# Row-phase order for the conv results, the residual and the identity of a two-layer conv kernel

## The chip, the cores and the metric

The kernel runs on one core of a Trainium2 chip. The metric is the device time of one execution in microseconds (us). The kernel before took 3264.07 us, the median of three runs (3260.51 to 3272.7).

A core has a tensor engine (PE in the profile, with its weight loads shown apart as PEld), a vector engine (VectorE, DVE), a scalar engine (ScalarE, ACT), GpSimd (POOL) and a sync engine (SP) that here only issues transfers (DMAs). Each runs its own list of instructions in order and waits on semaphores of the others. The transfers of all queues run on the same 16 DMA engines.

## The reference, cut to what matters

The input x is 4 images of 128 channels x 128 x 128 pixels, float32. Two layers follow each other.

The first layer has an attention over 9 x 9 overlapping 16 x 16 regions per image (step 14) with a residual; the overlaps are averaged. Its result is called `xf`. Then:

```python
y = _ln(xf, ln2_g, ln2_b)
y = y @ w_p0 + b_p0                      # 128 -> 256 channels
ym = conv5x5_depthwise(ym, dw_k)         # padding 2
ym = batch_norm(ym)                      # mean and variance over all images and pixels
y = gelu(gelu(ym)) @ w_p2 + b_p2         # 256 -> 128 channels
x = y + xf
```

The second layer keeps its input as identity:

```python
identity = x
out = act_quant(x)                       # clip to 0..1, 15 levels
out = conv3x3(out, weight_quant(w1))
out = act_quant(batchnorm(out, gamma1, beta1))
out = conv3x3(out, weight_quant(w2))
return batchnorm(out, gamma2, beta2) + identity
```

(The names are shortened from the reference; both batch norms need the statistics of the whole batch before any of their output can be formed.)

## The kernel before, in words

The order of the work on PE, ScalarE, VectorE and SP is the order in which the kernel's Python calls are made (`manual_schedule`); no planner moves instructions there. Channels lie on the 128 partitions. The line numbers are those of the kernel before.

**Attention and depthwise conv.** The attention runs over 36 bands of 16 rows. `beside(t)` (L881) lays the projections of the neighbouring bands and pieces of the depthwise conv between the attention's products. `post_chunks` (L528) ends a band: the merged rows go out to the memory tensor `xf_d` (through the list of stores that L431 issues on SP), the first 256-channel projection goes to `y2_d`, split into even and odd columns. Two tiles per half hold that projection on its way out, so ScalarE must wait for a store to land before it reuses one.

The depthwise conv (`conv_steps`, L614, matmuls in `depthwise`, L600) is a banded product. An image's 128 rows are cut into groups g of 16 rows. Partitions of its result are four channels times 32 values m = 2 ro + e, where ro is the row within the group and e says even or odd column; the free dimensions are the groups and the 64 columns x of that parity. So one result tile holds, for one (ro, e), the rows ro, ro + 16, ro + 32 and so on. Those of one ro are called a row phase here. `products` (L640) copies the result from PSUM, takes statistics, and stores it to `cv_d`. `conv_rest` (L678) does the last two groups of the last image when the attention is over; it has its own store loop (L729). `cv_d` is `[group, channel, (m, x)]`, so that a partition of the tile is written as one piece of 64 values (256 B) for each group.

**GELU stage** (`gelu_stage`, L1187). It works by units of 1024 pixels; there are 64, 16 per image, and a unit is eight neighbouring rows. For each: SP loads `cv` (1 MB, L1199) and `xfl` (0.5 MB, L1208), ScalarE does the batch norm with the first GELU and then the second GELU (L1216, L1219), PE projects (L1228), VectorE adds the residual and the even and odd columns fall back into place (L1236), GpSimd clips, VectorE quantises into a padded 8-bit image `q1[b]` of 130 x 130 (L1246, `to_int`, L1176). The identity goes to `id_d`. Two units behind, `conv3x3` (L1157) runs the first 3x3 conv: 18 matmuls per unit, nine for each half of four rows; tap t has its row offset dy = t // 3. `stats_of` (L1172) takes the statistics, `keep` (L1249) copies the result to `c1_d`, or, for the last image, to the on-chip tile `c1_s`.

**Last stages** (`last_stages`, L1287). The statistics pass (loop at L1317): unit n is loaded, normalised with Relu on ScalarE (L1328), and the second 3x3 conv of unit n - 3 runs on PE. On VectorE the calls stand in this order:

```python
                    pc = conv3x3(ps_d, n - 3, wq[1])
                    stats_of(st2, n - 3, pc)
...
                        nc.vector.tensor_scalar(a[:, px], a[:, px], 15.0, ROUND, ALU.min, ALU.add)
                        to_int(rows_in(q1[b], k)[:, h], a[:, px])
```

so the quantisation of unit n (L1340, L1176) comes after the statistics of the conv of unit n - 3. The conv result itself is dropped, except for the last image, whose results overwrite `c1_s`. Once the statistics are complete, the output pass (L1346) does the conv again for three images, applies the batch norm (ScalarE, L1350), adds the identity loaded from `id_d` up to eight units ahead (VectorE, L1351) and stores to `out` (L1354). Four PSUM tiles and four `z` tiles take turns.

Of the kernel before, what the change touches and what calls it, by code (L numbers as in the profile page):

```python
# [14 lines left out]
P = 128  # L15
# [14 lines left out]
N_TAPS = 25  # L30
MAX_SCORE = 64.0
GR = 16
CW = P // 2
KD = 2 * (GR + 4)
NCK = 8
# [11 lines left out]
def layers(  # L47
# [40 lines left out]


    y2_d = [dram.tile([P + 4, 2, 2 * P, CW], F32, name=f"y2_d{b}") for b in range(B)]  # L90
    cv_d = [dram.tile([P // GR, 2 * P, GR * P], F32, name=f"cv_d{b}") for b in range(B)]

    dw_d = dram.tile([2 * NCK, KD, 3, 16 * 32], F32, name="dw_d")
    pad_d = dram.tile([2 * GR + 3, 7, 2 * P], F32, name="pad_d")
# [90 lines left out]
    with ExitStack() as actx:  # L185
# [342 lines left out]
        def post_chunks(t, sel=None):  # L528


            b, i = bands[t]
            chunks = []
            for at, (r, n) in enumerate(finished(t)):
                held = {}
                squares, variance, deviation, spread, scaled = normalise(
                    lambda n=n, held=held: held["xf"][:, : n * P], n * P, sel
                )

                def project(hh, r=r, n=n, at=at, held=held):
                    if hh == 0:  # L540
                        held["xf"] = xfp.tile([P, LB * P], F32, name="xf")
                    px = slice(hh * n // 2 * P, (hh + 1) * n // 2 * P)
                    pm = ps_m.tile([P, 512], F32, name="pm")
                    po = pm[:, : n // 2 * P]
                    nc.tensor.matmul(po, wo, rows_of(ob[t], r + hh * n // 2, n // 2), start=True, stop=True)  # L545
                    nc.vector.scalar_tensor_tensor(
                        held["xf"][:, px], po, bo, xr[t, at][:, px], ALU.add, ALU.add
                    )
                    if hh:
                        store(  # L550
                            xf_d[b][:, (i * STEP + r) * P : (i * STEP + r + n) * P],
                            held["xf"][:, : n * P],
                        )
# [60 lines left out]
        def conv_steps(n, ahead=2):  # L614
# [25 lines left out]
            def products(at):  # L640
                k, jj, c0 = tiles[at]
                ut, wt = U.pop(at), W[k, jj]
                pc = [ps_m.tile([P, nj, ng, CW], F32, name="pm") for _ in range(2)]
                depthwise(pc, wt[:, :, c0:], ut, nc_)
                for half in range(2):
                    cv = cp.tile([P, nj, ng, CW], F32, name=f"c{half}")
                    nc.scalar.copy(  # L647
                        cv.rearrange("p j g x -> p (j g x)"), pc[half].rearrange("p j g x -> p (j g x)")
                    )
                    for j in range(nj):  # L650
                        nc.vector.bn_stats(  # L651
                            st0[:, k, half, 2 * jj + c0 // 4 + j, n, :], cv[:, j].rearrange("p g x -> p (g x)")
                        )
                        ch = 32 * k + 16 * half + 8 * jj + c0 + 4 * j
                        store(
                            bass.AP(
                                cv_d[b].tensor,
                                cv_d[b][g0, ch, 0:1].offset,
                                [[CW, P], [2 * P * GR * P, ng], [1, CW]],
                            ),  # L660
                            cv[:, j],
                        )

            def begin():
# [13 lines left out]
        def conv_rest(n, w_t, u_t, c_t):  # L678
# [32 lines left out]
            def step(k):  # L711
# [6 lines left out]
                for half in range(2):  # L718
# [6 lines left out]
                            st0[:, k, half, j, n, :], cv[:, j].rearrange("p g x -> p (g x)")  # L725
                        )
                    engine = (nc.sync, nc.scalar)[half]
                    for g in range(ng):
                        engine.dma_start(  # L729
                            out=bass.AP(  # L730
                                cv_d[b].tensor,
                                cv_d[b][g0 + g, 32 * k + 16 * half, 0:1].offset,
                                [[CW, P], [4 * GR * P, 4], [1, CW]],
                            ),
                            in_=cv[:, :, g],
                        )

            def run_all():
                for k in range(4):
# [400 lines left out]
    def padded(pool, name):  # L1140
        q = pool.tile([P, QW, QW], F8, name=name)
        nc.gpsimd.memset(q[:, 0, :], 0.0)
        nc.gpsimd.memset(q[:, QW - 1, :], 0.0)
        nc.gpsimd.memset(q[:, 1 : QW - 1, 0:1], 0.0)
        nc.gpsimd.memset(q[:, 1 : QW - 1, QW - 1 :], 0.0)
        return q

    U = 2 * RB * P
    units = [(b, k) for b in range(B) for k in range(NU2)]

    def pixels(k):
        return slice(k * U, (k + 1) * U)

    def rows_in(q, k):
        return q[:, 1 + 2 * RB * k : 1 + 2 * RB * (k + 1), 1 : 1 + P]

    def conv3x3(pool, n, w):  # L1157
        b, k = units[n]
        pc = pool.tile([P, 2, RB, P], F32, name="pc")
        for h in range(2):  # L1160
            r = (2 * k + h) * RB
            for t in range(9):
                dy, dx = divmod(t, 3)
                nc.tensor.matmul(  # L1164
                    pc[:, h], w[:, t, :], q1[b][:, r + dy : r + dy + RB, dx : dx + P],
                    start=(t == 0), stop=(t == 8),
                )
        return pc.rearrange("p h r c -> p h (r c)")
# [18 lines left out]
    def gelu_stage():  # L1187
        with (
# [7 lines left out]
            def load(n):  # L1196
# [1 line left out]
                cv = ld.tile([P, 2, U], F32, name="cv")  # L1198
                nc.sync.dma_start(  # L1199
                    out=cv,  # L1200
                    in_=cv_d[b][k // 2].rearrange("(h p) n -> p h n", p=P)[:, :, pixels(k % 2)],
                )
                loaded[n] = [cv]

# [16 lines left out]
            def second_projection(n):  # L1221
# [12 lines left out]
                pb_ = pb.rearrange("p m n -> p (m n)").rearrange("p (r e c) -> p r e c", e=2, c=P // 2)  # L1234
# [12 lines left out]
                to_int(rows_in(q1[b], k), a)  # L1247

            def keep(n, pc):  # L1249
                b, k = units[n]  # L1250
# [9 lines left out]
            gelus(0)  # L1260
            before1()
            before2()
            for n in range(len(units) + 2):
                if n + 2 < len(units):
                    load(n + 2)
                    load_xf(n + 2)
# [10 lines left out]
                if n >= 2:  # L1277
                    stats_of(st1, n - 2, pc)
                    keep(n - 2, pc)
                if n == len(units) - 1:  # L1280
                    most1()
            for out_, in_ in stores:
# [4 lines left out]
    def last_stages():  # L1287
        with (
# [18 lines left out]
                    nc.sync.dma_start(out=firsts[n], in_=c1_d[b][:, pixels(k)])  # L1307

            def load_id(at):
                b, k = units[order[at]]  # L1310
# [6 lines left out]
            for n in range(len(units) + 3):  # L1317
# [10 lines left out]
                        nc.scalar.activation(a[:, px], a[:, px], AF.Relu, bias=sh1, scale=sc1)  # L1328

                if n >= 3:  # L1330
                    b, k = units[n - 3]
# [12 lines left out]
            sc2, sh2 = rest2()  # L1344
            stores = []
            for at, n in enumerate(order):  # L1346
                b, k = units[n]
# [59 lines left out]
```

## Time and profile before

| | |
|---|---|
| median of three runs | 3264.07 us |
| span of the profiled execution | 3262.4 us |
| PE busy | 3089.8 us (95%), 30,954 matmuls |
| VectorE, ScalarE, GpSimd busy | 2018.7, 1991.5, 837.6 us |
| moved by DMA | 680.65 MB in 809,828 packets |
| packets under 512 B, under 2 KB, under 8 KB | 580,919, 695,936, 809,472 |
| mean rate | 209 GB/s |

The profiled execution's own time is its span, within 1.7 us of the median of the runs. Busy PE time is the time in which a matmul is under way; matmuls are pipelined, so a busy PE isn't PE at its peak. The counts of packets are cumulative: 580,919 of the 809,828 carry less than 512 B. The profile also cuts the span into 40 slices of 81.6 us, where a digit is the busy share in tenths, and it can be asked for any window. A line such as "PE pm L600 <- DMA u<-y_d: 16.6, 6, 5.4" says that PE's work of line 600 waited for that transfer 16.6 us in all, 6 times, at most 5.4 us.

### The profile page before, as it was taken

To read this page: it belongs to the slowest core of one execution; us is meant where nothing else is said; L and a number is where in the kernel's file an instruction comes from. 1 tells how busy PE (TensorE), PEld (TensorE's weight loads), DVE (VectorE), ACT (ScalarE), POOL (GpSimd) and SP (SyncE) were. 2 spreads that over 40 slices of the span, in tenths; PEclk is the share of its full clock that TensorE was granted. 3 is DMA by queue.
4 is the path that set the end of the run, shared out by engine and by line. 5 is a ranking of instruction groups with operands and counts; after the bars stand their busy time and mean duration, and the time that the engine had idled before them with its cause. 6 is when DMAs were issued, how large, how long until landed. Compare 5 with 4: busy or idle time off the path is not lost.

```text
span 3262.4 us, 75716 instructions
## 1 busy us (share of the span) xinstructions
PE 3089.8 (95%) x30954; PEld 1544.8 (47%) x30954; DVE 2018.7 (62%) x3244; ACT 1991.5 (61%) x2658; POOL 837.6 (26%) x1058
## 2 busy tenths in 40 slices
PE   8999999999999999999989998876899999999998
PEld 4555554544544444544444444443544444444443
DVE  5877887776766667676655564542555555666543
ACT  5777776777776776767655564532467777433443
POOL 3444443333333333333322232211111111000000
PEclk9999999999999999999999998877699999999999
DMA  3555677888886888886889988857899999552398
GB/s 82 150 165 159 170 185 183 192 210 198 208 200 160 193 202 204 197 209 166 188 203 207 201 199 187 191 158 199 245 359 358 357 359 306 169 167 84 106 357 312
DMA packets 809828, 680.65 MB, mean 209 GB/s; under 512 B 580919, under 2 KB 695936, under 8 KB 809472
## 3 DMA queue, kind: packets, MB, share of 16 engines
q1 hardware_dynamic: 798879, 669.17, 75.6%
q8 instruction: 247, 4.05, 0.5%
q0 software_dynamic: 1024, 3.93, 0.4%
q10 hardware_dynamic: 9568, 2.61, 0.3%
q14 instruction: 110, 0.89, 0.1%
HBM read 408.72 MB, written 270.79 MB: 208 GB/s over the span
## 4 chain that ended last, share of the span: by engine, by line
PE 80%; DMA 7%; issue 4%; ACT 4%; SPq 3%; DVE 3%; POOL 0%; ACTq 0%; DVEq 0%; POOLq 0%
PE pc L1164 21%; PE pm L600 9%; PE sc L784 9%; PE po L847 8%; PE pm L493 7%; PE pb L1228 7%; PE pm L561 5%; PE pm L770 4%; PE po L855 4%; DMA y_d<-y 3%; PE pm L377 3%; PE pm L545 3%; ACT pt L792 2%; DVE rd L867 1%; DMA u<-y_d 1%
## 5 line engine op out<-in xcount | busy, mean ns | idle before, releaser
L867 DVE RECIPROCAL rd<-po 128x256 f32<-128x256 f32 x324 | 569.3, 1757 | 447.6 <-PE po L855 444.7
L792 ACT ACTIVATE pt<-sc 128x1024 f32<-128x1024 f32 x648 | 628.0, 1024 | 128.2 <-PE sc L784 62.6
L1164 PE MATMUL pc<-q,wq 128*128 128x512 fp8e4 x3168 | 699.0, 380 | 5.1 <-DVE q L1176 5.1
L802 POOL TENSOR_TENSOR sm<-pt 128x512 f32<-128x512 f32 x324 | 413.2, 1275 | 1058.2 <-ACT pt L792 718.3
L1164 PEld LDWEIGHTS <-wq 128*128 128x128 fp8e4 x3168 | 308.7, 97 | 405.7 <-issue 37.0
L784 PE MATMUL sc<-q,kr 32*128 32x256 f32 x5184 | 403.3, 414 | 22.5 <-ACT pt L792 22.2
L600 PE MATMUL pm<-u,w 40*32 40x504 f32 (+5 forms) x7680 | 372.0, 505 | 45.6 <-DMA u<-y_d 22.5
L784 PEld LDWEIGHTS sc<-q,kr 32*128 32x128 f32 x5184 | 249.6, 190 | 261.8 <-issue 166.7
L847 PE MATMUL po<-pt,v 128*32 128x256 f32 x5184 | 358.9, 396 | 5.5 <-DVE part L871 4.7
L647 ACT COPY c<-pm 128x512 f32<-128x512 f32 (+1 forms) x256 | 132.3, 563 | 280.2 <-PE pm L600 249.4
L561 PE MATMUL pm<-xn,wp 128*128 128x512 f32 (+1 forms) x576 | 250.1, 565 | 38.1 <-ACT y L566 37.5
L566 ACT ACTIVATE y<-pm,vectors 128x512 f32<-128x512 f32 (+1 forms) x288 | 182.9, 641 | 152.4 <-DMA y_d<-y 98.3
L802 DVE TENSOR_TENSOR sm<-pt 128x512 f32<-128x512 f32 x324 | 243.7, 752 | 29.8 <-ACT pt L792 29.8
L600 PEld LDWEIGHTS pm<-u,w 40*32 40x32 f32 x7680 | 146.4, 112 | 229.9 <-issue 163.3
L493 PE MATMUL pm<-xn,wqkv 128*128 128x512 f32 (+1 forms) x576 | 248.5, 560 | 2.7 <-ACT v L775 2.0
L651 DVE BATCH_NORM_STATS2 st<-c 128x6 f32<-128x512 f32 (+2 forms) x320 | 160.9, 550 | 142.1 <-ACT c L647 141.7
L1228 PE MATMUL pb<-cv,wp 128*128 128x512 f32 x512 | 232.8, 598 | 4.9 <-ACT cv L1219 4.9
L847 PEld LDWEIGHTS po<-pt,v 128*32 128x32 f32 x5184 | 139.2, 111 | 177.9 <-issue 102.8
L1172 DVE BATCH_NORM_STATS2 st<-pc 128x6 f32<-128x512 f32 x256 | 165.8, 690 | 83.4 <-PE pc L1164 83.4
L855 PE MATMUL po<-sm,ones 128*32 128x256 f32 x2592 | 204.1, 386 | 0.8 <-issue 0.8
L770 PE MATMUL pm<-wqkv,yr 128*128 128x128 f32 x1296 | 192.8, 290 | 0.0
L770 PEld LDWEIGHTS pm<-wqkv,yr 128*128 128x128 f32 x1296 | 158.5, 191 | 67.6 <-issue 44.0
(157 smaller groups left out, 3438.3 us busy)
## 6 DMA issues: line engine op xcount, KB each, us to landing
cv<-cv_d SPq DMA_DIRECT2D x64, 1024.0 KB
u<-y_d SPq DMA_DIRECT2D x234, 256.0 KB
cv_d<-c SPq DMA_DIRECT2D x192, 256.0 KB
y_d<-y SPq DMA_DIRECT2D x160, 256.0 KB
xn<-row SPq DMA_DIRECT2D x76, 512.0 KB
xfl<-xf_d SPq DMA_DIRECT2D x64, 512.0 KB
id_d<-y SPq DMA_DIRECT2D x64, 512.0 KB
idt<-id_d SPq DMA_DIRECT2D x64, 512.0 KB
```

The source lines that it names most:

```text
L493: nc.tensor.matmul(pm[:, : n * P], wqkv[:, m * P : (m + 1) * P], held["xn"][hh], start=True, stop=True,)
L561: nc.tensor.matmul(pm[:, : n * P], wp0[:, h, :], held["xn"][hh], start=True, stop=True)
L600: nc.tensor.matmul(outs[half][32 * q : 32 * q + 32, j, :, a:z], wt[hs, s, c, :], ut[hs, :, c, a + s - 1 : z + s - 1], start=(s == 1), stop ...
L770: nc.tensor.matmul(pv[:, m, c, :], region(yr, j + m)[:, c * P : (c + 1) * P], wqkv[:, 2 * P :], start=True, stop=True,)
L784: nc.tensor.matmul(sc[h // 2][:, h % 2, kc, :].rearrange("p (r c) -> p r c", c=RS), region(kr, j)[hs, kc * P : (kc + 1) * P], queries(j, h ...
L792: nc.scalar.activation(pt, sc[p], AF.Exp)
L802: add(sm, pt[:, :, 0, :], pt[:, :, 1, :], ALU.add)
L847: nc.tensor.matmul(po[hs, 0, :], v[:, kc, hs], pt[h // 2][:, h % 2, kc, :], start=(kc == 0), stop=(kc == 1),)
L855: nc.tensor.matmul(po[hs, 1, :], ones, sm[h // 2][:, h % 2, :], start=True, stop=True)
L867: nc.vector.reciprocal(rd, po[:, 1, :])
L1164: nc.tensor.matmul(pc[:, h], w[:, t, :], q1[b][:, r + dy : r + dy + RB, dx : dx + P], start=(t == 0), stop=(t == 8),)
L1228: nc.tensor.matmul(pb[:, m], wp2[:, h, :], cv[:, h, px], start=(h == 0), stop=(h == 1))
```

## The change

The tensors in memory between the stages get the order of the row phases. `cv_d` becomes `[channel, m, group, x]`, so a partition of a conv result is one piece of all its groups: 8 x 64 values where a tile holds eight groups, 4 x 64 or 2 x 64 in the last image's parts. `xf_d`, `id_d` and `c1_d` keep their shape but hold the rows in the order (phase, group): the eight rows k, k + 16, ..., k + 112 of phase k are 1024 values in a row. `xf` is still produced in blocks of natural rows, so it is stored row by row, and a block that straddles a multiple of 16 takes two stores.

A unit of the late stages is now the eight rows of one phase. A 3x3 conv of phase k needs the phases k - 1, k and k + 1; for phase 0 the neighbour above is phase 15 one group up, and for phase 15 the one below is phase 0 one group down. The padded image is laid out by phases: a zero row, phase 15, phase 0, a zero row, phases 1 to 14 (`first_row`), so each tap still reads four rows that lie together. Units are quantised in the order 15, 0, 1, ..., 14 (`units`), and convs go 0 to 15 (`conv_units`). In the GELU stage the conv now runs three units behind instead of two; in the statistics pass it stays at three. The output is stored as eight rows that lie 16 rows apart.

```diff
-    cv_d = [dram.tile([P // GR, 2 * P, GR * P], F32, name=f"cv_d{b}") for b in range(B)]
+    cv_d = [dram.tile([2 * P, 32, P // GR, CW], F32, name=f"cv_d{b}") for b in range(B)]
...
                     if hh:
-                        store(
-                            xf_d[b][:, (i * STEP + r) * P : (i * STEP + r + n) * P],
-                            held["xf"][:, : n * P],
-                        )
+                        row = i * STEP + r
+                        cut = min(n, GR - row % GR)
+                        for a, z in ((0, cut), (cut, n)):
+                            if z > a:
+                                g, ro = divmod(row + a, GR)
+                                store(
+                                    xf_d[b].rearrange("p (o g c) -> p o g c", o=GR, c=P)[
+                                        :, ro : ro + z - a, g, :
+                                    ],
+                                    held["xf"][:, a * P : z * P].rearrange("p (r c) -> p r c", c=P),
+                                )
...
                                 cv_d[b].tensor,
-                                cv_d[b][g0, ch, 0:1].offset,
-                                [[CW, P], [2 * P * GR * P, ng], [1, CW]],
+                                cv_d[b][ch, 0, g0, 0:1].offset,
+                                [[P // GR * CW, P], [1, ng * CW]],
...
-                    for g in range(ng):
-                        engine.dma_start(
...
-                                cv_d[b][g0 + g, 32 * k + 16 * half, 0:1].offset,
-                                [[CW, P], [4 * GR * P, 4], [1, CW]],
...
+                    engine.dma_start(
...
+                            cv_d[b][32 * k + 16 * half, 0, g0, 0:1].offset,
+                            [[P // GR * CW, P], [4 * P * P, 4], [1, ng * CW]],
...
-    units = [(b, k) for b in range(B) for k in range(NU2)]
+    units = [(b, (k - 1) % GR) for b in range(B) for k in range(GR)]
+    conv_units = [(b, k) for b in range(B) for k in range(GR)]
...
+    def first_row(k):
+        return {-1: 0, GR - 1: 1, 0: NG + 1, GR: NG + 2}.get(k, NG + 2 + NG * k)
+
     def rows_in(q, k):
-        return q[:, 1 + 2 * RB * k : 1 + 2 * RB * (k + 1), 1 : 1 + P]
+        return q[:, first_row(k) : first_row(k) + NG, 1 : 1 + P]
 
     def conv3x3(pool, n, w):
-        b, k = units[n]
+        b, k = conv_units[n]
         pc = pool.tile([P, 2, RB, P], F32, name="pc")
         for h in range(2):
-            r = (2 * k + h) * RB
             for t in range(9):
                 dy, dx = divmod(t, 3)
+                r = first_row(k + dy - 1) + h * RB
                 nc.tensor.matmul(
-                    pc[:, h], w[:, t, :], q1[b][:, r + dy : r + dy + RB, dx : dx + P],
+                    pc[:, h], w[:, t, :], q1[b][:, r : r + RB, dx : dx + P],
...
-                    in_=cv_d[b][k // 2].rearrange("(h p) n -> p h n", p=P)[:, :, pixels(k % 2)],
+                    in_=cv_d[b].rearrange("(h p) m g x -> p h (m g x)", p=P)[:, :, pixels(k)],
...
-                        odd_even(y)[:, :, e], pb_[:, :, e, :], bp2, odd_even(xf)[:, :, e], ALU.add, ALU.add
+                        odd_even(y)[:, :, e], pb[:, e], bp2, odd_even(xf)[:, :, e], ALU.add, ALU.add
...
-            for n in range(len(units) + 2):
+            for n in range(len(units) + 3):
...
-                if n >= 2:
-                    pc = conv3x3(ps_c, n - 2, wq[0])
+                if n >= 3:
+                    pc = conv3x3(ps_c, n - 3, wq[0])
...
-                    out=out[b, :, 2 * RB * k : 2 * RB * (k + 1), :].rearrange("c r w -> c (r w)"), in_=z
+                    out=out[b, :, k:P:GR, :], in_=z.rearrange("p (r w) -> p r w", w=P)
```

The zero rows of `padded` move with the layout, and `keep`, `load_id` and the convs of the last stages take their unit from `conv_units`.

More of the change, by code (lines that the diff above doesn't have):

```diff
@@ L32 @@
 GR = 16
+NG = P // GR
 CW = P // 2
@@ L657, in products @@
                                 cv_d[b].tensor,
-                                cv_d[b][g0, ch, 0:1].offset,
-                                [[CW, P], [2 * P * GR * P, ng], [1, CW]],
+                                cv_d[b][ch, 0, g0, 0:1].offset,
+                                [[P // GR * CW, P], [1, ng * CW]],
                             ),
-                            cv[:, j],
+                            cv[:, j].rearrange("p g x -> p (g x)"),
                         )
@@ L727, in step @@
                     engine = (nc.sync, nc.scalar)[half]
-                    for g in range(ng):
-                        engine.dma_start(
-                            out=bass.AP(
-                                cv_d[b].tensor,
-                                cv_d[b][g0 + g, 32 * k + 16 * half, 0:1].offset,
-                                [[CW, P], [4 * GR * P, 4], [1, CW]],
-                            ),
-                            in_=cv[:, :, g],
-                        )
+                    engine.dma_start(
+                        out=bass.AP(
+                            cv_d[b].tensor,
+                            cv_d[b][32 * k + 16 * half, 0, g0, 0:1].offset,
+                            [[P // GR * CW, P], [4 * P * P, 4], [1, ng * CW]],
+                        ),
+                        in_=cv.rearrange("p j g x -> p j (g x)"),
+                    )
             def run_all():
@@ L1142, in padded @@
         nc.gpsimd.memset(q[:, 0, :], 0.0)
-        nc.gpsimd.memset(q[:, QW - 1, :], 0.0)
-        nc.gpsimd.memset(q[:, 1 : QW - 1, 0:1], 0.0)
-        nc.gpsimd.memset(q[:, 1 : QW - 1, QW - 1 :], 0.0)
+        nc.gpsimd.memset(q[:, 2 * NG + 1, :], 0.0)
+        nc.gpsimd.memset(q[:, :, 0:1], 0.0)
+        nc.gpsimd.memset(q[:, :, QW - 1 :], 0.0)
         return q
     U = 2 * RB * P
-    units = [(b, k) for b in range(B) for k in range(NU2)]
+    units = [(b, (k - 1) % GR) for b in range(B) for k in range(GR)]
+    conv_units = [(b, k) for b in range(B) for k in range(GR)]
     def pixels(k):
         return slice(k * U, (k + 1) * U)
+    def first_row(k):
+        return {-1: 0, GR - 1: 1, 0: NG + 1, GR: NG + 2}.get(k, NG + 2 + NG * k)
     def rows_in(q, k):
-        return q[:, 1 + 2 * RB * k : 1 + 2 * RB * (k + 1), 1 : 1 + P]
+        return q[:, first_row(k) : first_row(k) + NG, 1 : 1 + P]
     def conv3x3(pool, n, w):
-        b, k = units[n]
+        b, k = conv_units[n]
         pc = pool.tile([P, 2, RB, P], F32, name="pc")
         for h in range(2):
-            r = (2 * k + h) * RB
             for t in range(9):
                 dy, dx = divmod(t, 3)
+                r = first_row(k + dy - 1) + h * RB
                 nc.tensor.matmul(
-                    pc[:, h], w[:, t, :], q1[b][:, r + dy : r + dy + RB, dx : dx + P],
+                    pc[:, h], w[:, t, :], q1[b][:, r : r + RB, dx : dx + P],
                     start=(t == 0), stop=(t == 8),
@@ L1233, in second_projection @@
                 odd_even = lambda t: t.rearrange("p (n e) -> p n e", e=2)
-                pb_ = pb.rearrange("p m n -> p (m n)").rearrange("p (r e c) -> p r e c", e=2, c=P // 2)
                 for e in range(2):
                     nc.vector.scalar_tensor_tensor(
-                        odd_even(y)[:, :, e], pb_[:, :, e, :], bp2, odd_even(xf)[:, :, e], ALU.add, ALU.add
+                        odd_even(y)[:, :, e], pb[:, e], bp2, odd_even(xf)[:, :, e], ALU.add, ALU.add
                     )
@@ L1249, in keep @@
             def keep(n, pc):
-                b, k = units[n]
+                b, k = conv_units[n]
                 c = c1_s[:, pixels(k)] if b == B - 1 else bw.tile([P, U], F32, name="c1")
@@ L1272, in gelu_stage @@
                 a = second_projection(n) if n < len(units) else None
-                if n >= 2:
-                    pc = conv3x3(ps_c, n - 2, wq[0])
+                if n >= 3:
+                    pc = conv3x3(ps_c, n - 3, wq[0])
                 if a is not None:
                     quantise(n, a)
-                if n >= 2:
-                    stats_of(st1, n - 2, pc)
-                    keep(n - 2, pc)
+                if n >= 3:
+                    stats_of(st1, n - 3, pc)
+                    keep(n - 3, pc)
                 if n == len(units) - 1:
@@ L1309, in load_id @@
             def load_id(at):
-                b, k = units[order[at]]
+                b, k = conv_units[order[at]]
                 idt[at] = idp.tile([P, U], F32, name="idt")
@@ L1330, in last_stages @@
                 if n >= 3:
-                    b, k = units[n - 3]
+                    b, k = conv_units[n - 3]
                     pc = conv3x3(ps_d, n - 3, wq[1])
@@ L1346, in last_stages @@
             for at, n in enumerate(order):
-                b, k = units[n]
+                b, k = conv_units[n]
                 pc = conv3x3(ps_d, n, wq[1]).rearrange("p h n -> p (h n)") if b < B - 1 else c1_s[:, pixels(k)]
```

## The prediction

> **What bounds the kernel now.** I read the slices first, then busy time by stage, then the chain of work that ended last, then VectorE's own timeline inside one stage, then PE's waits.
>
> The slices: PE is at 8 or 9 tenths nearly everywhere, so a saving counts only where it removes a PE wait, and a new PE wait counts in full.
>
> ```profile
> PE   8999999999999999999989998876899999999998
> DMA  3555677888886888886889988857899999552398
> ```
>
> Busy time by stage (PE, PEld, DVE, ACT, POOL, each with its count; then PE clock, DMA share, GB/s):
>
> ```profile
> 530.00:1580.00 1050.00, 1031.93 (x12161) 517.13 (x12160) 731.49 (x1132) 746.82 (x1125) 379.49 (x482) 1.00 0.83 195
> 1580.00:2230.00 650.00, 574.28 (x8360) 300.98 (x8344) 343.37 (x602) 338.07 (x531) 153.94 (x194) 0.90 0.83 192
> 2230.00:2334.00 104.00, 67.66 (x1627) 52.28 (x1626) 37.46 (x166) 25.05 (x41) 12.60 (x26) 0.63 0.77 202
> 2334.00:2814.00 480.00, 473.13 (x1665) 209.62 (x1665) 262.66 (x399) 332.34 (x259) 71.62 (x78) 0.99 0.93 329
> 2814.00:3065.00 251.00, 251.00 (x1153) 112.34 (x1152) 167.02 (x260) 90.77 (x78) 0.00 (x0) 1.00 0.37 111
> 3065.00:3262.40 197.40, 187.56 (x865) 83.86 (x863) 79.35 (x70) 76.89 (x65) 0.55 (x1) 0.99 0.89 320
> ```
>
> Attention with the depthwise conv beside it ends at 2230, the rest of that conv at 2334, the GELU stage at 2814, the first pass of the second 3x3 conv (its statistics) at 3065; the output pass follows. In the two 3x3 passes PE never waits, and the chain says so in one piece, 2016 matmuls in 438.95 us, 0.2177 us each:
>
> ```profile
> 2813.62 438.95 PE pc L1164 x2016
> ```
>
> In the statistics pass VectorE repeats this, 3.91 us per unit (unit start, us, operation; the bracket is its idle time and releaser):
>
> ```profile
> 2885.44 1.29 DVE L1172 BATCH_NORM_STATS2 st<-pc 128x6 f32<-128x512 f32 x2 [1.28 <-PE pc L1164]
> 2886.66 0.68 DVE L1340 TENSOR_SCALAR c1l<-c1l 128x1024 f32<-128x1024 f32 x1
> 2887.37 0.70 DVE L1176 TENSOR_SCALAR q<-c1l 128x1024 fp8e4<-128x1024 f32 x1
> 2889.35 1.30 DVE L1172 BATCH_NORM_STATS2 st<-pc 128x6 f32<-128x512 f32 x2 [1.28 <-PE pc L1164]
> ```
>
> Both statistics wait for the end of a conv, and the quantisation of a unit stands behind them. From the start of the statistics to the end of L1176 it is 2888.07 - 2885.44 = 2.63 us.
>
> In 1580 to 2230 PE does wait, and mostly for transfers:
>
> ```profile
> PE pm L600 <- DMA u<-y_d: 16.6, 6, 5.4
> ```
>
> (that line is for 1960 to 2230 alone).
>
> **What the Trainium skill says.** "DMA: Bandwidth & Descriptors", section "Why small descriptors are slow (HBM only)": a fixed cost of some 3 cycles per packet makes short ones dear. The trace's packet records agree: median 18 ns (mean 19) for 256 B, 27 for 512 B, 53 for 1024 B, 84 for 2048 B, 159 for 4096 B. The 512 B ones are 640 loads at the start; no 512 B store is there. Same page, "Latency and other measured facts": a row pitch of 512 KiB or more per partition slows copies. The cv loads go from a pitch of 8 KiB to 64 KiB, below what the page lists; the output pass already moves everything at 64 KiB and reaches 357 GB/s in its full slices, so I charge nothing. [...]half-clock stretches of 3.413, 6.827, 10.24 us, each after a window in which PE was busy for at most 0.62 of it; windows as low as 0.58 also passed without a drop.
>
> **The change, part by part.**
>
> *Stores of the depthwise result.* 262,144 packets of 256 B become 24,576 of 2048 B (three images), 8,192 of 1024 B and 16,384 of 512 B (the last image's parts). Before: 262,144 x 19 ns / 16 engines = 311 us of DMA time. After: (24,576 x 84 + 8,192 x 53 + 16,384 x 27) / 16 = 184 us. The xf stores go the other way: 5,120 packets of 4096 B and 4,096 of 3072 B (121 ns) become 65,536 of 512 B, 82 us becoming 111, and 20 more issues on SP (five row blocks per image straddle a multiple of 16) at 0.34 us, 7 us in all on a queue that mostly waits. Net -98 us out of some 1,490 DMA-busy us in 530 to 2334. What of it is on the path: in 530 to 1580 PE idles 18 us in pieces of mostly under 1 us; I take -3. In 1580 to 2230 the saving is 114,688 x 19/16 = 136 us against 84, less 9 for xf: 43 of 540 busy us, 8%. There PE idles 76 us, and a mean clock of 0.90 means 130 us at half clock, up to 65 us lost: a pot of 141. The chain there has y2 stores, u loads and cv stores of 3 to 9 us, mostly queueing, but also round trips and SP order, which shorter packets don't touch. I take -30, between 0 and -70. In 2230 to 2334 the conv remainder issues 16 DMAs instead of 32, and its packets take 14 us instead of 18: -2.
>
> *GELU stage.* The sum of projection and residual, the casts and the 4 KB loads keep their counts and sizes. PE paces it: 8 x 0.429 + 18 x 0.217 = 7.34 us per unit. The 3x3 conv now runs three units behind. Its need for the newest quantised unit moves from its 16th to its 7th matmul, 2 us earlier; in this stage VectorE quantises before the statistics (done at 2507.31, the next conv's 7th matmul at about 2511.8), so 4.4 us of slack hide it. At the start one more unit has no conv beside it: ScalarE's two GELUs take 2.36 + 1.91 us per unit, and the fourth projection could not start before 2351.2, while PE would be free at 2347.9: +3.5. The extra conv at the end is the same work, moved. The queue of id and c1 stores on SP moves with it, and nobody waits for them before the next stage.
>
> *Statistics pass: the new wait.* Here the lag stays at three units, but the unit that conv m needs last is no longer m+1, for its last three matmuls, but m+2, phase k+1, for its 7th (the third row of taps, in both halves). In the built program's order the wait on VectorE does stand before the 16th matmul in the kernel before and before the 7th now. Unit m+2 is quantised behind the statistics of conv m-1, which is the conv just before it on PE. So each conv: starts at N; statistics start at N + 0.2 (the gap between the next matmul's start and VectorE's start in the GELU stage); quantisation ends at N + 0.2 + 2.63; a matmul follows a released wait by 0.05 us (2813.57 to 2813.62); so the 7th starts at N + 2.88 instead of N + 6 x 0.217 = N + 1.30. Stall 1.58 us. Behind it on PE are the other 11 matmuls, for which the next statistics wait, so it repeats and cannot be caught up. Phases 14 and 15 need nothing that late: 14 of 16 units stall, 56 less the first: 55 x 1.58 = +87. Nothing hides it. The start of the pass needs a third unit quantised before the 7th matmul: +2. c1 loads and Relu (1.24 us) get more time per unit, so they stay hidden.
>
> *Output pass.* Stores of 8 rows become 1,024 packets of 512 B instead of 128 of 4096 B. DMA work: 56 loads x 128 x 170 ns/16 = 76 us, and stores 64 x 1,024 x 27/16 = 111 (before, 64 x 128 x 170/16 = 87). 187 us, from about 6 us in, against a stage of 197 with PE 188: nearly even with PE, so some waits and a longer tail. A 512 B store isn't in the trace: at the loads' 27 ns it costs about 0, at twice the 256 B price (36 ns) 223 + 6 - 197 = +32. I take +8, since 27 is the nearest row.
>
> Sum: -3 - 30 - 2 + 3.5 + 87 + 2 + 8 = +65.5. On the profiled span of 3262.4 us: 3328. The median of the runs is 1.7 us above that span: **3330**, 2% slower.
>
> **The rivals.**
>
> *Stall and half clock (0.22).* A 3.413 us window that holds a whole stall is filled to 0.54 by start times, 0.58 if the last matmul's drain counts: where the trace has both drops and none. If it drops, about 40% of the pass runs at half clock, where a unit takes 2.88 + 12 x 0.427 = 8.0 us instead of 5.5: about 0.8 us more on 56 units, +44: 3374.
>
> *Store-bound output pass (0.10).* 36 ns a packet: +24 on my sum, 3354.
>
> *Shorter queues buy nothing (0.07).* The stores do not land sooner, or the round trips set the waits: 3330 + 35 = 3365.
>
> *Not slower (0.07).* Place: 1580 to 2230. Mechanism: with 8% less DMA work the 3 to 6 us PE gaps fall under the point where the clock drops, and both go. It decides if 100 of the 141 us come back: 3260, and at 120 it is 3240. Against it: the gaps also come from row/xn round trips and SP's order.
>
> The likeliest case gets 0.54, with its own range 3305 to 3350.
>
> **Numbers.** This kernel's runs spread by 0.4%, so 0.5% is about what tells a change from none. Faster than 3248: 0.04; within 0.5%: 0.03, both out of the last rival; slower: 0.93. The range runs from 3292 (an attention gain near 70) to 3385 (half clock and a little store cost).
>
> **What would show it.** Right: between the GELU stage and the output pass PE idles about 87 us in some 55 pieces of 1.6, all before a conv matmul and released by L1176's counterpart; the pass takes about 340 us; packets under 512 B fall by 262,144. Wrong: no such gaps (some slack that I missed), PE clock at half there (the first rival), or 1580 to 2230 shorter by 100.

## The result and the profile after

The changed kernel took 3344.34 us (median of four runs, 3342.27 to 3349.96) against 3264.87 for the kernel before on the same chip: a ratio of 1.0241, with a 95% interval from 1.0222 to 1.0261. It is 2.4% slower. The forecast was 3330, in a range from 3292 to 3385.

The slices of the changed kernel's page, PE and DMA, as of 83.6 us each:

```profile
PE   8999999999999999999999999767999998777898
DMA  3555677878776787876788878676999994431299
DMA packets 710564, 680.66 MB, mean 204 GB/s; under 512 B 318838, under 2 KB 589503, under 8 KB 710207
```

The attention shows no new hole. The new one is near the end, three slices at 7 with an 8 on either side, where the page before had 9. The number of packets under 512 B fell from 580,919 to 318,838, by 262,081: the small stores are gone as the change says.

Busy time by stage, with the stages cut where this kernel's begin (same columns as before):

```profile
1580.00:2213.00 633.00, 567.59 (x8383) 299.88 (x8376) 347.25 (x608) 338.62 (x533) 155.89 (x198) 0.91 0.78 199
2213.00:2324.00 111.00, 67.46 (x1627) 51.95 (x1625) 37.59 (x166) 24.76 (x41) 11.95 (x26) 0.60 0.70 188
2324.00:2804.00 480.00, 472.91 (x1664) 209.40 (x1664) 261.86 (x396) 331.89 (x258) 72.01 (x78) 0.99 0.92 329
2804.00:3148.00 344.00, 265.05 (x1172) 113.57 (x1173) 170.11 (x269) 92.79 (x81) 0.55 (x1) 0.99 0.27 81
3148.00:3342.10 194.10, 183.49 (x846) 81.83 (x844) 76.97 (x64) 75.79 (x64) 0.00 (x0) 0.98 1.00 325
```

The statistics pass is now 344 us long with 265 us of PE work in it. Before, it was 251 us with 251. Its own timeline (start, us, engine and operation, count; the bracket is the idle time of the engine and its releaser):

```profile
2907.15 1.29 DVE L1188 BATCH_NORM_STATS2 st<-pc 128x6 f32<-128x512 f32 x2 [2.86 <-PE pc L1180]
2908.36 0.68 DVE L1355 TENSOR_SCALAR c1l<-c1l 128x1024 f32<-128x1024 f32 x1
...
2909.07 0.70 DVE L1192 TENSOR_SCALAR q<-c1l 128x1024 fp8e4<-128x1024 f32 x1
...
2909.82 4.07 PE L1180 MATMUL pc<-q,wq 128*128 128x512 fp8e4 x18 [1.41 <-DVE q L1192]
...
2912.62 1.30 DVE L1188 BATCH_NORM_STATS2 st<-pc 128x6 f32<-128x512 f32 x2 [2.85 <-PE pc L1180]
...
2915.30 4.07 PE L1180 MATMUL pc<-q,wq 128*128 128x512 fp8e4 x18 [1.41 <-DVE q L1192]
```

(In the numbering of the changed kernel L1180 is the 3x3 conv, L1188 the statistics, L1192 the quantisation into the padded image.) The quantisation ends at 2909.77, and 0.05 us later PE goes on; it runs 18 matmuls, from the 7th of one conv to the 6th of the next, and stops again. The period is 5.48 us where it was 3.91. The bracket says 1.41 and not 1.58 because the profile counts the drain of the last matmul, by the difference 0.17 us, as busy. In the list of PE's waits this is the longest (first line below); the kernel before has the second line in its place:

```profile
PE pc L1180 <- DVE q L1192: 83.4, 57, 5.1
```

```profile
PE pc L1164 <- DVE q L1176: 5.1, 1, 5.1
```

57 waits: 55 of 1.41 us, one of 5.1 at the head of the pass, which the kernel before has too, and one of 0.9 behind it.

So that the runs can be compared by stage, here are five times of each profiled execution: the last depthwise matmul beside the attention (that is, the length of the attention part), from there to the first projection of the GELU stage, to the first Relu of the statistics pass, to the first batch norm of the output pass, and to the end.

| kernel | attention | conv remainder | GELU | statistics pass | output | span |
|---|---|---|---|---|---|---|
| before | 2225.6 | 108.0 | 478.2 | 257.2 | 193.4 | 3262.4 |
| changed | 2208.8 | 115.2 | 478.8 | 345.2 | 194.1 | 3342.1 |
| difference | -16.8 | +7.2 | +0.6 | +88.0 | +0.7 | +79.7 |

### The profile page after: what moved, and what is told of

Read it like the earlier page. It is cut to its first block, busy times and chain, and to the rows that moved or that the text cites. A ratio compares the mean times of both kernels' runs of the same rounds, so it can differ in the third digit from the quotient of the medians.

```text
span 3342.1 us, 75730 instructions
## 1 busy us (share of the span) xinstructions
PE 3093.3 (93%) x30954; PEld 1542.8 (46%) x30954; DVE 2018.4 (60%) x3244; ACT 1990.5 (60%) x2658; POOL 836.7 (25%) x1058
## 2 busy tenths in 40 slices
DMA packets 710564, 680.66 MB, mean 204 GB/s; under 512 B 318838, under 2 KB 589503, under 8 KB 710207
## 3 DMA queue, kind: packets, MB, share of 16 engines
q0 software_dynamic: 1024, 3.93, 0.4%
## 4 chain that ended last, share of the span: by engine, by line
PE 80%; DVE 6%; DMA 6%; issue 4%; ACT 3%; SPq 1%; ACTq 0%; POOL 0%; POOLq 0%; DVEq 0%
PE pc L1180 19%; PE pm L608 10%; PE sc L791 9%; PE po L854 9%; PE pm L494 6%; PE pb L1244 6%; PE pm L569 6%; PE pm L777 5%; PE po L862 4%; PE pm L378 3%; PE pm L546 3%; DVE st L1188 2%; DMA y_d<-y 2%; DMA u<-y_d 1%; DVE q L1192 1%
## 5 line engine op out<-in xcount | busy, mean ns | idle before, releaser
L1180 PE MATMUL pc<-q,wq 128*128 128x512 fp8e4 x3168 | 708.5, 380 | 83.4 <-DVE q L1192 83.4
L799 ACT ACTIVATE pt<-sc 128x1024 f32<-128x1024 f32 x648 | 627.8, 1024 | 128.4 <-PE sc L791 58.4
L1180 PEld LDWEIGHTS <-wq 128*128 128x128 fp8e4 x3168 | 307.4, 97 | 494.7 <-issue 131.6
L1188 DVE BATCH_NORM_STATS2 st<-pc 128x6 f32<-128x512 f32 x256 | 165.7, 689 | 174.1 <-PE pc L1180 174.1
L777 PE MATMUL pm<-wqkv,yr 128*128 128x128 f32 x1296 | 193.4, 290 | 0.0
```

The lines of the kernel that those rows point to most:

```text
L777: nc.tensor.matmul(pv[:, m, c, :], region(yr, j + m)[:, c * P : (c + 1) * P], wqkv[:, 2 * P :], start=True, stop=True,)
L799: nc.scalar.activation(pt, sc[p], AF.Exp)
L1180: nc.tensor.matmul(pc[:, h], w[:, t, :], q1[b][:, r : r + RB, dx : dx + P], start=(t == 0), stop=(t == 8),)
```

## The experiments

Each ratio is to the kernel before as run on the same chip beside the experiment; its median there was between 3260 and 3269 us, so medians of different experiments are compared through their ratios.

**The order on VectorE.** In the statistics pass the two quantising instructions were put ahead of the statistics.

```diff
                 if n >= 3:
-                    b, k = conv_units[n - 3]
                     pc = conv3x3(ps_d, n - 3, wq[1])
-                    stats_of(st2, n - 3, pc)
-                    if b == B - 1:
-                        nc.scalar.copy(c1_s[:, pixels(k)], ...)
                 if n < len(units):
...
                         to_int(rows_in(q1[b], k)[:, h], a[:, px])
+                if n >= 3:
+                    b, k = conv_units[n - 3]
+                    stats_of(st2, n - 3, pc)
+                    if b == B - 1:
+                        nc.scalar.copy(c1_s[:, pixels(k)], ...)
```

> The changed kernel, with the two quantising instructions of a unit put ahead of the statistics of the conv in the statistics pass. Theory (the stall comes from VectorE's order: statistics of conv m-1, then the unit that conv m waits for): all 55 stalls of 1.58 us go, the pass falls from 343 to about 256 us, the time from 3344 to about 3257 us, and PE waits for the quantisation only at the start of the pass. Rival (PE is slower on the new layout itself: its reads of the phase-ordered rows, or the wait at the 7th matmul whatever stands before it): the time stays within 10 us of 3344. Against the kernel before: 0.2% faster, since the attention part keeps its 17 us and the rest of the depthwise conv its 7 us loss.

Measured: 3262.4 us, a ratio of 1.0008 (0.9995 to 1.0022) to the kernel before. The loss of 2.4% is gone, with every layout of the change in place, so PE isn't slower on the phase-ordered rows. But it wasn't the 3257 forecast: the statistics pass took 271.2 us instead of 256. In its first three quarters PE waits only at the head; in the last image it waits again, by this timeline of the run:

```profile
3000.48 4.07 PE L1180 MATMUL pc<-q,wq 128*128 128x512 fp8e4 x18 [0.83 <-DVE q L1192]
...
3001.72 1.01 ACT L1357 COPY c_s<-pc 128x1024 f32<-128x1024 f32 x1 [2.75 <-DVE st L1188]
3002.63 1.24 ACT L1343 ACTIVATE c_s<-c_s,shift,scale 128x1024 f32<-128x1024 f32 x1
3003.91 0.69 DVE L1351 TENSOR_SCALAR c_s<-c_s 128x1024 f32<-128x1024 f32 x1 [2.27 <-ACT c_s L1343]
```

For the last image ScalarE copies each conv result into the on-chip tile `c1_s`. That copy waits for the statistics, the next unit's Relu stands behind the copy, the quantisation waits for the Relu, and the next statistics stand behind the quantisation. This is a loop again, of VectorE and ScalarE this time, with a period of 4.90 us, 1 us more than PE needs. It comes 13 times, and PE shows 11 of them as waits of 0.83 us. I had not looked at ScalarE's order.

**One conv more of distance.** The other cure leaves the order alone and lets the conv run four units behind.

```diff
-            for n in range(len(units) + 3):
+            for n in range(len(units) + 4):
...
-                if n >= 3:
-                    b, k = conv_units[n - 3]
-                    pc = conv3x3(ps_d, n - 3, wq[1])
-                    stats_of(st2, n - 3, pc)
+                if n >= 4:
+                    b, k = conv_units[n - 4]
+                    pc = conv3x3(ps_d, n - 4, wq[1])
+                    stats_of(st2, n - 4, pc)
```

> The changed kernel with the conv of the statistics pass four units behind instead of three, the statistics still ahead of the quantisation. Theory: the unit that conv m needs is then quantised behind the statistics of conv m-2, which PE finished a whole conv earlier, so no stall either: about 3257 us, equal to the kernel with the order swapped within 5 us. Rival (the position of the wait alone): no change from 3344.

Measured: 3253.27 us, ratio 0.9975 (0.9964 to 0.9987), with a statistics pass of 259.2 us. The wait still stands before the 7th matmul, but what it waits for is done a conv earlier, so the position of the wait alone costs nothing. The whole change with this one number altered is 0.25% faster than the kernel before. Two of PE's waits for the quantisation are left, both at the head of the pass:

```profile
PE pc L1180 <- DVE q L1192: 6.0, 2, 5.1
```

**The 16th matmul.** The kernel before, with its lag cut from three to two, also has its newest unit quantised behind the statistics of the conv just ahead.

```diff
-            for n in range(len(units) + 3):
+            for n in range(len(units) + 2):
...
-                if n >= 3:
-                    b, k = units[n - 3]
-                    pc = conv3x3(ps_d, n - 3, wq[1])
-                    stats_of(st2, n - 3, pc)
+                if n >= 2:
+                    b, k = units[n - 2]
+                    pc = conv3x3(ps_d, n - 2, wq[1])
+                    stats_of(st2, n - 2, pc)
```

> The kernel before with the conv of its statistics pass two units behind instead of three, so that its newest unit too is quantised behind the statistics of the conv just ahead, but is needed at the 16th matmul. Theory: the wait is over at N + 2.88 us and the 16th matmul comes at N + 15 x 0.217 = N + 3.26, so 0.4 us of slack are left and the time stays within 0.2% of the kernel before. Rival (every wait on a unit quantised behind the last statistics stalls PE): 1.5 us on 60 units, about 3350 us.

Measured: 3263.56 us, ratio 1.0015 (1.0001 to 1.0028); the statistics pass took 257.6 us against 257.2. No stall: at the 16th matmul 0.4 us of slack is enough. It is the two things together that cost, the distance of one conv and the early need.

**The 13th matmul.** Here the changed kernel's taps were reordered so that the row from the newest unit comes last for both halves.

```diff
-        for h in range(2):
-            for t in range(9):
+        for taps, h in ((range(6), 0), (range(6), 1), (range(6, 9), 0), (range(6, 9), 1)):
+            for t in taps:
```

> The changed kernel with the taps of all convs reordered: the first two tap rows of both halves, then the third row of both, so the wait stands at the 13th matmul of 18 instead of the 7th. Theory: stall = 2.88 - 12 x 0.217 = 0.28 us a unit instead of 1.58, but the first half's accumulation ends later, which the statistics don't feel as they wait for the whole conv: 55 x 1.30 = 72 us less, about 3273 us. Rival (layout, not the wait): 3344.

Measured: 3269.13 us, ratio 1.0026 (1.0014 to 1.0038); the statistics pass took 275.1 us, 70 less than the changed kernel's 345.2, for 72 forecast. The trace has 55 waits of 0.11 us, again 0.17 us less than the stall because of the drain. So the stall does follow the arithmetic 2.88 us less 0.217 us for each matmul ahead of the wait: 1.58 at the 7th, 0.28 at the 13th, none at the 16th.

**The conv stores alone, and the xf stores alone.** Each was put by itself into the kernel before, with the stores of the change and the loads left flat.

```diff
-    cv_d = [dram.tile([P // GR, 2 * P, GR * P], F32, name=f"cv_d{b}") for b in range(B)]
+    cv_d = [dram.tile([2 * P, 32, P // GR, CW], F32, name=f"cv_d{b}") for b in range(B)]
...
+                                [[P // GR * CW, P], [1, ng * CW]],
...
+                    in_=cv_d[b].rearrange("(h p) m g x -> p h (m g x)", p=P)[:, :, pixels(k)],
```

> The kernel before with the order of cv_d alone changed: the conv results are stored in pieces of 2048, 1024 and 512 B, and the late stages load the flat units from it as before, so the pixels of that tensor reach them in the wrong order (that part of the computation is changed; all else is as before). Theory: the cv stores made the whole attention gain, about 20 us up to the last attention-stage matmul, and the one-piece stores of the conv remainder made its loss of 7 us; the rest is unchanged: 3260 - 13 = about 3247 us. Rival (the gain or the loss comes from the xf stores): no change from 3260.

```diff
-                            xf_d[b][:, (i * STEP + r) * P : (i * STEP + r + n) * P],
...
+                                    xf_d[b].rearrange("p (o g c) -> p o g c", o=GR, c=P)[
+                                        :, ro : ro + z - a, g, :
+                                    ],
```

> The kernel before with the order of xf_d alone changed: 72 stores become 92, in packets of 512 B, and the residual reaches the late stages in the wrong pixel order (that part is changed; all else is as before). Theory: 29 us more DMA time spread over the attention and 20 issues on SP cost 0 to 5 us: 3260 to 3265. Rival (SP's order and its lanes set the waits, so 20 more issues cost as much as 100 us of DMA time): 10 us or more, 3270.

Measured: the conv stores alone give 3246.43 us, ratio 0.9944 (0.9927 to 0.996). The xf stores alone give 3275.49, ratio 1.0027 (1.0014 to 1.0041). By stage:

| kernel | attention | conv remainder | GELU | statistics pass | output |
|---|---|---|---|---|---|
| conv stores alone | 2199.8 | 115.7 | 477.3 | 257.3 | 195.5 |
| xf stores alone | 2230.9 | 112.1 | 478.2 | 258.4 | 193.3 |
| changed, quantisation first | 2197.9 | 115.8 | 479.1 | 271.2 | 194.1 |
| changed, four units behind | 2206.1 | 114.6 | 479.6 | 259.2 | 194.1 |
| changed, taps reordered | 2208.2 | 114.1 | 480.2 | 275.1 | 194.4 |
| before, two units behind | 2222.1 | 107.0 | 478.5 | 257.6 | 193.3 |

The attention's code is the same in the changed kernel, its three variants here and the one with two stores below: 2197.9 to 2213.3, mean 2206.9. That is also how far one execution can be trusted. The kernel before and its variant have a mean of 2223.9. So the whole change gives the attention 17 us. The conv stores alone give 24, and the xf stores alone take 7; each of these is one execution, and the 7 lies within the spread just given. The answer is between the two expectations for xf: the ratio is worth 9 us in all, more than the 0 to 5 of the theory, a little less than the 10 of the rival.

PE's waits show the largest part of the 17 us. From 530 us to the end of the attention, before (first block) and after (second):

```profile
PE pm L561 <- ACT y L566: 25.7, 14, 4.9
PE pm L600 <- DMA u<-y_d: 22.5, 11, 5.4
```

```profile
PE pm L608 <- DMA u<-y_d: 26.5, 16, 6.5
PE pm L569 <- ACT y L574: 10.0, 6, 2.8
```

What fell is PE's wait for ScalarE's `y`, the projection that needs a store to land before its tile is free. The waits for the loads of `u` did not fall.

**How much the attention follows the DMA load.** Half of the conv stores beside the attention were left out.

```diff
+                        if half:
+                            continue
                         store(
...
+                for h in range(2):
+                    nc.sync.dma_start(
+                        out=cv[:, h],
...
+                            [[32 * P * P, 8], [P * P, 16], [1, U]],
```

> The changed kernel with the statistics pass four units behind, leaving out half of the conv stores beside the attention (those of the second 16 of each 32 channels; the late stages read the first 16 twice, in two loads a unit). It takes some 90 us of DMA time and half of the store issues away from the attention. If the waits there follow the DMA load, the attention part falls by another 15 us or more, as the 98 us that the change took away gave 17; if they are round trips and SP's order, by 5 at most. The GELU stage keeps its bytes and should stay at 479 us.

Measured: 3385.3 us, ratio 1.0376 (1.031 to 1.0443), and that total says nothing on the question, because the GELU stage took 627.3 us instead of the 479 expected. Its loads were built here with an outermost dimension of 8. The Trainium skill ("DMA: Bandwidth & Descriptors", "Why a DMA increments its semaphore by 16 and not by 1") says that a transfer uses the largest number of engines up to 16 that divides the outermost dimensions of both of its sides, here 8 and 128, so 8 engines. The trace agrees: in the window from 2400 to 2800, with a DMA share of 0.76 and 266 GB/s, 8 or 9 packets are under way for 46% of the time. In the changed kernel, from 2340 to 2780 with 0.96 and 344 GB/s, that holds for 0.4%. These loads also come in two where the changed kernel has one; no run has that alone.

The attention part, which ends before those loads, took 2178.2 us, 29 less than the mean of 2206.9. The packets from 530 us to the first projection take 1310 us of the 16 engines' time, 70 less than in the kernel four units behind (1380) and not 90, and PE's time at half clock up to the end of the attention fell from 126 to 88 us. So the waits there still follow the conv stores. That it is their DMA time that counts isn't shown: the edit also takes 160 of their 320 issues off SP, and the whole change gave only 17 us for 105 us of DMA time.

**Two stores per half in the conv remainder.**

```diff
-                    engine.dma_start(
...
-                            [[P // GR * CW, P], [4 * P * P, 4], [1, ng * CW]],
+                    for g in range(ng):
+                        engine.dma_start(
...
+                                [[P // GR * CW, P], [4 * P * P, 4], [1, CW]],
```

> The changed kernel with the statistics pass four units behind, and in the conv remainder two stores of 256 B pieces per half again instead of one of 512 B pieces. Theory (the one-piece stores, or the place that they take among the transfers SP waits for, made the remainder 7 us longer): the stretch from the last attention-stage conv matmul to the first projection falls from 115 to 108 us, the time from 3253 to about 3246. Rival (the remainder is longer because it starts with a fuller DMA queue or the xf stores ahead of it): no change, 3253.

Measured: 3252.88 us, ratio 0.9964 (0.995 to 0.9978), against 0.9975 (0.9964 to 0.9987) with one store: the intervals overlap. The remainder took 111.9 us, halfway. Its products alone took 48.9 us, as in the kernel before (48.7), where the changed kernel has 54.0 and the same kernel with one store 51.3, so the store shape looked like the cause of some 2 to 5 us. The last pair below tested that.

**The best of the parts.** xf in natural rows again, loaded by rows, with four units of distance; and the same with two stores in the remainder.

```diff
...
-                nc.sync.dma_start(out=xf, in_=xf_d[b][:, pixels(k)])
+                nc.sync.dma_start(
+                    out=xf.rearrange("p (g c) -> p g c", c=P),
+                    in_=xf_d[b].rearrange("p (g o c) -> p g o c", o=GR, c=P)[:, :, k, :],
+                )
```

> The changed kernel, four units behind in the statistics pass, with xf_d in natural rows again: 72 stores in packets of 3 and 4 KB, and the late stages load a phase's eight rows in pieces of 512 B. Theory: the attention keeps the whole gain of the cv stores (ends near 2200 us, 6 earlier than with xf in phase order), and the GELU stage stays at 479 us, since 1,024 packets x 28 ns/16 = 1.8 us of loads instead of 1.5 leave its DMA share just under full: about 3246 us, 0.5 to 0.6% under the kernel before. Rival: the loads' extra 0.3 us a unit makes the GELU stage DMA-bound, 64 x 0.3 = 20 us longer, and nothing is gained: 3265.

> The same with two stores per half in the conv remainder. Theory (with one store per half, SP's next loads of u wait for the store that it has just issued, 25 us in all instead of 11): the remainder's products take 48.7 us again instead of 51 to 54, 4 us less in all: about 3242 us. Rival (that difference is of the state of the DMA queue): as the run beside it, within 1 us in that stretch.

Measured: 3251.96 us, ratio 0.9948 (0.9928 to 0.9968), and 3246.01 us, ratio 0.9936 (0.9917 to 0.9956). Both are faster than the kernel before, by 0.5 and 0.6%, and can't be told from each other. The attention ended at 2193.5 and 2196.7, 12 us under the mean with xf in phase order. The GELU stage took 479.7 and 479.3 us: the 512 B loads cost nothing there.

The remainder, though, refuted its theory. SP's waits between 2235 and 2325, first with one store and then with two:

```profile
SPq L690 <- DMA cv_d<-c: 25.0, 5, 6.6
```

```profile
SPq L690 <- DMA cv_d<-c: 11.8, 3, 6.1
```

The waits of the u loads for conv stores fell from 25 to 12 us as expected, and the products still took 52.7 us against 52.3. So those waits were not what made the remainder longer. The store shape may still have a part in it: in the profiles of the other four kernels with two stores the products took 48.6 to 49.5 us, in the seven with one store 51.3 to 54.0, and this last run is the one exception. Each of these is a single execution, and the cause stays open.

## Why the prediction was right

- **The new wait in the statistics pass** was forecast at +87 and +2, and the pass grew by 88.0 us. The step's parts hold one by one: the stall sits before the 7th matmul, ends with the quantisation, comes 55 times at 1.58 us in the period (5.48 against 3.91), goes when the order or the distance is altered, and shrinks or goes when the matmul that needs the unit comes later. The four runs show that as the cause.
- **The half clock** did not come. The record has full clock from 2809.7 us, 7 us into the pass, to the last matmul, through windows of 3.413 us that by start times are filled to 0.54 in the worst case (3.413 - 1.58 of 3.413). That rival fell at the point where the trace of before could not decide.
- **The attention** was forecast at -33 and gave -17. The DMA time fell as forecast: the packets from 530 us to the first projection take 1385 us of the 16 engines' time instead of 1490, 105 less for 98. One price in that sum was misread: 53 ns is not the median for 1024 B, which is 71 ns over 81,097 packets. The step that was mis-sized is what PE gets of the DMA time. PE's idle time from 530 us to the end of the attention fell from 94 to 78 us, but its time at half clock stayed (130 and 126 us), so of the pot of 141 us only idle time came back. The parts moved the same way. In the proportions of the forecast's 52 us saved and 9 us lost, its -30 is, as an estimate, -36 for the conv stores and +6 for xf. The runs give -24 to -29 for the conv stores, and +7 (alone) to +12 (the two natural-row kernels against the rest) for xf.
- **The conv remainder** was forecast at -2 and gave +7. That step had the wrong sign. xf alone lengthens it by 4, the conv stores alone by 8; why is open. The theory of SP's waits was tried and fell.
- **The GELU stage** was forecast at +3.5 and gave +0.6: three units of distance hide the earlier need as argued (no such wait shows in the stage). For the start I took the time of the fourth projection from the trace of before, where ScalarE had waited 2.44 us for that unit's load of `cv`. In the changed kernel that wait is 0.66 us, and PE idles 1.27 us ahead of the fourth projection. The kernel before idles 0.70 us ahead of its fifth, at 2360, where the changed one doesn't, which leaves about 0.6 us.
- **The output pass** was forecast at +8 and gave +0.7. The price of a 512 B store, bounded from 27 to 36 ns, is 27.1 (mean of the 65,536 packets of the pass). The DMA share there is 1.00, and yet no wait of PE shows in the pass; only ScalarE waits for a store, twice, 3.5 us in all. That the identity tiles loaded up to eight units ahead and the last z tiles take up what PE would have waited for is my reading, which no run tests.
- **Shorter queues buy nothing** and **not slower** both fell: the attention did get shorter, but by 17 us and not by 100.

The one large term was right within 1 us. The sum missed by 14 us: the attention and the remainder came out 16 and 9 us worse than forecast, the output pass and the GELU stage 7 and 3 us better. That these partly cancel is luck.

## What to carry to other kernels

When a pipeline's data dependency moves, count the distance in the order of the engine that makes the operand, not in loop iterations: "three units behind" was one spare conv before and none after, because the producer now stands behind a consumer of the conv just issued. The stall is the producer's chain less what the waiting engine can do before the first instruction that needs it, and a step more of distance removes it, and a later need shrinks or removes it; swapping the producer's order also removes it, if no other engine (here ScalarE with its copy) closes a loop of its own. And of a layout change that trades small stores for others, run each tensor by itself: here the conv stores gained 0.6%, the xf stores lost 0.3%, and reading xf in small pieces where PE sets the pace was free.

## What I had not expected of the hardware

A store of 512 B pieces costs the same per packet as a load, 27.1 ns against 27 in the profile, and the output pass ran with DMA engines busy all the time (share 1.00) at 325 GB/s without a longer stage. A PE that idles 1.58 us in every 5.48 kept its full clock from 2809.7 us to the end of the pass. And loads whose outermost dimension was 8 came with a GELU stage 148 us longer for the same bytes, and with no more than 8 or 9 packets under way for 46% of the window from 2400 to 2800.
